# A planner with per-engine clocks in place of credits, attention sums through DRAM, and the residual's products moved ahead of the gates, in a one-core transformer block

## The chip, the cores and the metric

The kernel runs on one core of one Trainium2 chip. The metric is the device time of one execution in microseconds; the kernel before was run three times: 890.34, 892.4 and 892.6 us, median 892.4 us. The profile is of one further execution. Engines are named as in the profile: PE (matrix multiply), PEld (its weight loads), DVE (vector), ACT (scalar and activation), POOL (GpSimd), SP (the engine whose queue issues most of the DMAs).

## The reference, cut to what matters

The input is x of 8 batches, 512 tokens, 256 features, all in float32. The block is causal attention with 16 heads of 16 features, plus a "memory" term, then a residual and layer norm, then a mixture of 8 experts with the top 2 of 10 gates (two of them null), a residual and a second layer norm.

```
qkv = x @ qkv_w.T + qkv_b                      # 16 heads of 16
seq_out = softmax(causal(q k^T / 4)) v
lines   = exterior products of x and x shifted by one token, 6 numbers a head
M       = decayed sum over earlier tokens of outer(Jw, Jw)        # 6 x 6 a head
mem_score = mix of rd.M.rd and |rd.M|^2
gated   = mean over heads of sigmoid(mem_score * mem_scale) * sigmoid(x @ memg_w.T + memg_b)
x = layernorm(x + (seq_out + gated * (x @ memv_w.T + memv_b)) @ out_w.T + out_b)
w, sel = top_k(softmax(x @ gate_w.T + gate_b), 2)
x = layernorm(x + sum over e of w_e * (x @ expert_w[e] + expert_b[e]))
```

`gated` is one number a token, and it can be had only when the memory sums of all earlier tokens are done.

## The kernel before, in words

**Attention** is cut into 160 stints, ten for a pair of head groups (4 groups of 4 heads, 8 batches). Stint k computes two things (`products`, L202): plain scores of stint k (`mx`, L223), from which DVE takes each query's largest (`negmax` L258) while ACT copies the diagonal blocks out (`dia` L267), POOL masks them (L282) and DVE takes their largest a stint later (`negdia` L250); and, for the stint that is 8 behind (`LAG`), transposed scores with the largest already folded in (`sc`, L228), which ACT exponentiates (`pe`, L263) and POOL masks (L277). `mx` and `sc` have one buffer each of two PSUM banks, so that the next `mx` waits until `dia` is out. `values` (L296) multiplies `pe` with v, a column of ones beside it, into `po`.

**Attention's sums.** A group fills 32 rows for each of 4 heads: in groups with even number the first 16 rows are the sums and the next the denominator, in odd groups the other way round. ACT copies an even group's `po` to `osb` (L313), an odd one's to `raw`, and DVE merges it with a predicated copy (L316). The denominators alone (8 KB a group) go to DRAM (`den`, L314), come back spread over 128 partitions (`rec`, L323), are inverted on DVE (L325), go out again (`dr`, L327) and come back broadcast (`recs`, L664). POOL multiplies them in (L671).

**The other work** stands in Python generators: `memory` (lines, L399 to L442), `memory_sums` (64 rounds of two matmuls `pm` L560 with three DVE operations L568, L570, L550 and one POOL operation L531 each, 32 rounds for each half of the batches), `finish` and `memory_gate` (they end in `gated`), then for each batch `prepare` (L637: loads x, adds the output bias on POOL, multiplies in the denominators, and, once the gates of the half are known, adds gated * b2 on POOL, L676 and L677), `front` (L699: residual's products `pa` L708 and L711, added on DVE at L713 and L715, norm at L691, transposes `px`, gates of the experts) and `all_experts` (L803: 16 pairs of experts a batch, `pex` L827, each added by two DVE operations L831; then the second norm and the store).

**What sets the order.** The program order of every engine is fixed when the kernel is built (`in_this_order`). Between two stints `fill` (L900) runs generators on credit: a stint earns `TAKE` = 1.9 us less the price of what stands in it, plus 1.0 or 1.5; a generator yields the PE time that it used, or a word (`STEP`, `POOL`, `LESS`, `CALM`) that makes it go on at a later turn or when POOL has a share free. The prices are constants; no engine's load is followed. Credit that is not used becomes idle matmuls (`warm`, L894), one for each 0.3 us, which keep PE busy with nothing.

The last batches' experts run after the last stint.

Of the kernel before, what the change touches and what calls it, by code (L numbers as in the profile page):

```python
# [26 lines left out]
TAKE = 1.9  # L27
SB = 4
EARLY, MORE = 1.0, 1.5
WARM = 0.3  # L30
PV, PQ, PO = 1.2, 2.15, (1.05, 0.85, 0.65, 0.45)
ROUNDS = (2, 1)
BUCKET = 3
AHEAD = 6
HALF = 4
STEP, POOL, LESS = "goes on at the next turn", "needs GpSimd", "needs GpSimd for half as long"
CALM = "goes on at the next turn but a unit's last"
# [15 lines left out]
def in_pieces(op, *tiles):  # L53

    for c in range(0, NT, 2):
        op(*(t[:, c : c + 2] for t in tiles))
        yield STEP


def bc(ap, axis, n):  # L60

    ap = ap.unsqueeze(axis)
    shape = list(ap.shape)
    shape[axis] = n
    return ap.to_broadcast(shape)

# [12 lines left out]
def block_kernel(ctx, tc, x, xT, wqk, bqk, wtok, wod, memv, memvb, row, gw, we, eb, out):  # L79
    nc = tc.nc  # L80
    PS = bass.MemoryType.PSUM
    const = ctx.enter_context(tc.tile_pool(name="const", bufs=1))
    psA = ctx.enter_context(tc.tile_pool(name="psA", bufs=1, space=PS))
    psO = ctx.enter_context(tc.tile_pool(name="psO", bufs=1, space=PS))
    psB = ctx.enter_context(tc.tile_pool(name="psB", bufs=3, space=PS))
    att = ctx.enter_context(tc.tile_pool(name="att", bufs=2))
    dram = ctx.enter_context(tc.tile_pool(name="dram", bufs=2, space=bass.MemoryType.DRAM))
# [30 lines left out]
    memp = ctx.enter_context(tc.tile_pool(name="mem", bufs=1))  # L118
    lines_of = ExitStack()
    lp = lines_of.enter_context(tc.tile_pool(name="lines", bufs=2))  # L120
# [15 lines left out]
    make_identity(nc, ident)  # L136
# [12 lines left out]
    odd_rows = const.tile([P, 1], mybir.dt.uint8, name="odd_rows")  # L149
    nc.vector.tensor_copy(odd_rows, bq[:, 2 * NG + 1 : 2 * NG + 2])  # L150
# [145 lines left out]
    def values(u, *js):  # L296

        b, g = UNITS[u]
        if u not in pos:
            pos[u] = psO.tile([P, T], F32, tag="po", name=f"po{u}")  # L300
            begun[u] = set()
        for j in js:
            for h in range(4):
                nc.tensor.matmul(pos[u][32 * h : 32 * h + 32, j * P :], v_aug[b % 2][:, j, 4 * (g // 2) + h, g % 2 : g % 2 + 2].rearrange("p q d -> p (q d)"),  # L304
                                 pes[u, j, h // 2][:, h % 2], start=not begun[u], stop=len(begun[u]) == NT - 1)
            begun[u].add(j)
        if len(begun[u]) == NT:
            if g == 0:
                st[b]["osb"] = att.tile([P, KC, T], F32, name=f"osb{b}", tag="osb", bufs=3)
                st[b]["den"] = dram.tile([KC, 4, 2, T], F32, name=f"den{b}", tag="den")  # L310
            o = st[b]["osb"][:, g // 2, :]
            raw = att.tile([P, T], F32, name=f"raw{u}", tag="raw", bufs=1) if g % 2 else o
            nc.scalar.copy(raw, pos.pop(u))  # L313
            nc.sync.dma_start(st[b]["den"][g // 2, :, g % 2], raw[0 if g % 2 else DH :: 32])  # L314
            if g % 2:
                nc.vector.copy_predicated(o, odd_rows.to_broadcast([P, T]), raw)  # L316

    def invert(b, part):

        s = st[b]  # L320
        if part == 0:
            s["rec"] = att.tile([P, T // 8], F32, name=f"rec{b}", tag="rec", bufs=1)
            nc.sync.dma_start(s["rec"], s["den"].rearrange("k j q (e t) -> (k j q e) t", e=8))  # L323
        if part == 1:
            nc.vector.reciprocal(s["rec"], s["rec"])  # L325
            s["dr"] = dram.tile([KC, 8, T], F32, name=f"dr{b}", tag="dr")
            nc.sync.dma_start(s["dr"].rearrange("k j (e t) -> (k j e) t", e=8), s["rec"])  # L327


    def sigmoid(z):  # L330
# [3 lines left out]
        yield STEP  # L334
# [7 lines left out]
    def fold_values():  # L342

        wd, mv = wo, mv0
        for c in range(KC):
            pw = bank(f"pw{c}")
# [4 lines left out]
            yield 0.9  # L351
        for n in range(2):
            mbb = lp.tile([P, KC, P], F32, name="mbb")
# [8 lines left out]
            yield 0.9  # L362

    turned, lined, gates = set(), set(), set()
# [19 lines left out]
    def memory_later():  # L384
        for half in range(B // HALF):
            yield from memory_sums(half)

    finished, rounds = [], [0, 0]
    mem, lines_over = {}, []

    def lines(lp, b):
# [4 lines left out]
        for c in range(NT):  # L396
            pl = bank(f"pl{b}_{c}")
# [6 lines left out]
            yield 1.1  # L404

        nc.gpsimd.memset(s[0:1, 0, 0, : 4 * H], 0.0)
        nc.sync.dma_start(s[1:, :, 0, : 4 * H], w1[: P - 1])
        nc.sync.dma_start(s[0:1, 1:, 0, : 4 * H], w1[P - 1 :, : NT - 1])
        spawn(outer_lines(lp, b, s))

    def outer_lines(lp, b, s):
        t = mem[b // HALF]
        for _ in range(2):
            yield STEP
# [3 lines left out]
        yield POOL  # L418
# [5 lines left out]
        yield POOL  # L424
# [3 lines left out]
        yield POOL  # L428
# [3 lines left out]

        to = t["jw"][:, :, :, b % HALF, :6].rearrange("p c h k -> p c k h")
        nc.gpsimd.tensor_tensor(to[:, :, 0:3], lw[:, :, 0, 3:6], nw[:, :, 0, 3:6], ALU.subtract)
        nc.gpsimd.tensor_tensor(to[:, :, 3:6], lw[:, :, 0, 0:3], nw[:, :, 0, 0:3], ALU.subtract)
        yield STEP
        for v, o in ((t["rd"], t["rn"][:, :, :, b % HALF]), (t["jw"], t["jw"][:, :, :, b % HALF, 6])):
            sq = lp.tile([P, NT, H, 6], F32, name="sq", bufs=1)
            nc.scalar.activation(sq, v[:, :, :, b % HALF, :6], AF.Square)
            yield STEP  # L440
# [48 lines left out]
    def memory_ahead(half):  # L489
# [7 lines left out]
        yield STEP  # L497
        nc.vector.tensor_scalar(jl[96:, 0, :], jl[96:, 0, :], others[96:], None, ALU.mult)
        nc.sync.dma_start(jl[P - 1 :, 1:, :], dj[:, : NT - 1, :])
        yield STEP  # L500
        yield STEP
# [3 lines left out]
        yield POOL  # L505
# [4 lines left out]
        yield STEP  # L510
# [6 lines left out]
    def memory_sums(half):  # L517
# [24 lines left out]
        for n in range(AHEAD):  # L542
            outer(*todo[n])
            if n < 3:
                decay(*todo[n])
            if n % 2:
                yield STEP
# [5 lines left out]
        for n, (h, c) in enumerate(todo):  # L553
            h0 = h - h % 8
            if n % (4 * NT) == 0:
                rm = memp.tile([P, NT, 8 * HALF, 6], F32, tag="rm", name=f"rm{half}_{h0}", bufs=2)
            pm = bank(f"pm{half}_{h}_{c}")
# [6 lines left out]
            if n + AHEAD < len(todo):  # L564
                outer(*todo[n + AHEAD])
# [8 lines left out]
            yield 0.85  # L574
            if turn[0] != rounds[0]:
                rounds[:] = turn[0], 0
            rounds[1] += 1
            if rounds[1] >= ROUNDS[half]:
                yield STEP
            if n % (4 * NT) == 4 * NT - 1:  # L580
                sums(*behind)
                behind = None
                spawn(finish(half, h0, rm))

    def finish(half, h0, rm):
# [8 lines left out]
        for n, to, by in ((1, sm, of_heads), (2, sm2, rm)):  # L594
            for c in range(0, NT, 2):
                cs = slice(c, c + 2)
                yield LESS
# [5 lines left out]
        yield STEP  # L603
        nc.vector.tensor_reduce(*behind, AX.X, ALU.add)
        finished.append(half)
        if finished.count(half) == 2:
            spawn(memory_gate(half))

    def memory_gate(half):
        sm, sm2, rn, gexp = (mem[half][n] for n in ("sm", "sm2", "rn", "gexp"))  # L610
        if half == 0:
            al, be = memp.tile([P, 1], F32, name="al"), memp.tile([P, 1], F32, name="be")
            fac_of.update(al=al, be=be)
            nc.vector.tensor_copy(al, vec("mix"))
            yield from sigmoid(al)
            nc.vector.tensor_scalar(be, al, -1.0, 1.0, ALU.mult, ALU.add)
# [6 lines left out]
        yield STEP  # L623
# [3 lines left out]
        yield STEP  # L627
# [9 lines left out]
    def prepare(b):  # L637
        yield lambda: lines_over and b < left[0] + 3
        if not ffp:
            ffp.append(ctx.enter_context(tc.tile_pool(name="ff", bufs=2)))  # L640
# [9 lines left out]
        if len(ffp) == 2:  # L650
            ws = ffp[0].tile([P, KC, NTRUE, D], F32, name="ws", bufs=1)
            ffp.append(ws)
            for e in range(0, NTRUE, 2):
                for k in range(KC):
                    nc.sync.dma_start(ws[:, k, e : e + 2], we[e : e + 2, k * P : (k + 1) * P, :].rearrange("e p h -> p e h"))
                yield STEP
        for c in range(NT):
            yield LESS
            nc.gpsimd.tensor_tensor(xb[:, c], xb[:, c], ob2, ALU.add)
        yield lambda: b in done  # L660
        recs = []
        for k in range(KC):
            recs.append(ff.tile([P, T], F32, name=f"recs{b}_{k}", tag="recs"))
            nc.sync.dma_start(recs[k], bc(st[b]["dr"][k], 1, DH))  # L664
        yield STEP
        yield STEP
        for k in range(KC):
            for n in range(0, T, T // 2):
                yield LESS
                o = st[b]["osb"][:, k, n : n + T // 2]  # L670
                nc.gpsimd.tensor_tensor(o, o, recs[k][:, n : n + T // 2], ALU.mult)  # L671
        yield lambda: b // HALF in gates
        for c in range(NT):
            yield POOL
            gb2 = ff.tile([P, D], F32, tag="recs", name=f"gb2_{b}_{c}")
            nc.gpsimd.tensor_tensor(gb2, b2, gated[:, c, b : b + 1].to_broadcast([P, D]), ALU.mult)  # L676
            nc.gpsimd.tensor_tensor(xb[:, c], xb[:, c], gb2, ALU.add)  # L677
        yield STEP

    def root(mv, nm):  # L680

        n = mv.shape[1]
        rs = ffp[0].tile([P, NT], F32, tag="rs", name=f"rs_{nm}")
        nc.vector.tensor_scalar(rs[:, :n], mv[:, :, 1], EPS, None, ALU.add)  # L684
        rr = ffp[0].tile([P, NT], F32, tag="rr", name=f"rr_{nm}")
        nc.gpsimd.tensor_tensor(rr[:, :n], rs[:, :n], half[:, :n], ALU.pow)  # L686
        return rr

    def norm(out_t, in_t, mv, rr, c, r=None):
        r = c if r is None else r  # L690
        nc.vector.tensor_scalar(out_t[:, c, :], in_t[:, c, :], mv[:, c, 0:1], rr[:, r : r + 1],  # L691
                                ALU.subtract, ALU.mult)
# [6 lines left out]
    def front(b):  # L699

        yield lambda: b in prepared
        ff, osb, xb = ffp[0], st[b]["osb"], st[b]["xb"]
        y = xb
        mv = ff.tile([P, NT, 2], F32, tag="mv", name=f"mv1_{b}")
        for c in range(NT):
            pa = bank(f"pa{b}_{c}")
            for k in range(KC):
                nc.tensor.matmul(pa[:, D:], xt[:, b, k, c * P : (c + 1) * P], wt[:, k, CM : CM + D],  # L708
                                 start=(k == 0), stop=(k == KC - 1))
            for k in range(KC):  # L710
                nc.tensor.matmul(pa[:, :D], osb[:, k, c * P : (c + 1) * P], wo[:, k, :],  # L711
                                 start=(k == 0), stop=(k == KC - 1))
            nc.vector.scalar_tensor_tensor(y[:, c, :], pa[:, D:], gated[:, c, b : b + 1], xb[:, c, :],  # L713
                                           ALU.mult, ALU.add)
            nc.vector.tensor_tensor(y[:, c, :], y[:, c, :], pa[:, :D], ALU.add)  # L715
            stats(mv, y, c, f"a{b}")
            yield 1.9
        yield STEP
        x1 = y
        rr = root(mv, f"a{b}")  # L720
        yield STEP
        yield STEP
        for c in range(NT):
            norm(x1, y, mv, rr, c)
            if c % 2:
                yield STEP
        yield lambda: b < left[0] + 2
        x1T = ff.tile([P, KC, T], F32, tag="x1T", name=f"x1T_{b}")
        for k in range(KC):
            pt = bank(f"px{b}_{k}")  # L730
# [3 lines left out]
            yield 0.7  # L734

# [7 lines left out]
        yield 0.6  # L743
        yield STEP
# [8 lines left out]
        yield 0.3  # L753
        yield CALM
# [8 lines left out]
        for r in range(2):  # L763
# [16 lines left out]
            yield CALM  # L780
# [4 lines left out]
        yield CALM  # L785
# [9 lines left out]
        yield CALM  # L795
# [7 lines left out]
    def all_experts(b):  # L803
# [4 lines left out]
        yield STEP  # L808
# [5 lines left out]
        yield 0.4  # L814
# [219 lines left out]
```

## Time and profile before

| | us |
|---|---|
| median of 3 runs | 892.4 |
| the profiled execution | 894.46 |
| its span, first to last instruction | 892.7 |
| PE busy, and its idle matmuls (L898) alone | 810.6, 40.0 |
| DVE, ACT, POOL busy | 633.0, 365.3, 390.6 |
| last exponential of attention (L263) ends | 737.4 |
| first expert product (L827) starts | 372 |

A group of instructions is read as: line, engine, operation, what it writes and reads, shape, count; then the busy time of the group in us, the mean of one in ns; then the idle time of the engine just before these instructions, and what ended most of it. The clock that is granted to PE is a share of full speed; its mean over the span is 0.973.

### The profile page before, as it was taken

What the parts mean: (1) busy time and instruction counts of PE and PEld (TensorE: products, weight loads), DVE (VectorE), ACT (ScalarE), POOL (GpSimd) and SP (SyncE); (2) the same over time, 40 slices, a digit from 0 to 9 for tenths busy, and PEclk for the clock granted to TensorE, in tenths of its full rate; (3) what the DMA queues carried; (4) which work ended last, traced back from release to release, by engine and by line L of the source; (5) the groups of instructions that cost most, each with busy time, mean ns of one, the idle gap of its engine ahead of it and who ended that gap; (6) DMA issues with size and microseconds to landing.
All of it is one profiled execution on the core that took longest, in us unless ns stands there. A gap on an engine that the chain in (4) does not pass through costs nothing.

```text
span 892.7 us, 14145 instructions
## 1 busy us (share of the span) xinstructions
PE 810.6 (91%) x5102; PEld 444.6 (50%) x5102; DVE 633.0 (71%) x1431; ACT 365.3 (41%) x678; POOL 390.6 (44%) x695
## 2 busy tenths in 40 slices
PE   9999977887779998999898899999999998999997
PEld 5555545454546555644364346444644454545342
DVE  2445579897579677878576778766876847887765
ACT  4466664554545464353445354544454321000000
POOL 1265777584646496642133463344334425050000
PEclk9999998998999998999899999999999999999999
DMA  7000000300000010000001000020002002020000
GB/s 267 12 17 17 9 3 3 123 24 1 5 1 26 27 28 25 2 4 1 2 1 51 26 1 1 15 63 2 1 7 70 2 1 75 1 71 1 24 30 18
DMA packets 25846, 23.70 MB, mean 27 GB/s; under 512 B 8588, under 2 KB 21548, under 8 KB 25776
## 3 DMA queue, kind: packets, MB, share of 16 engines
q1 hardware_dynamic: 24432, 22.24, 8.1%
q8 instruction: 40, 0.66, 0.3%
q10 hardware_dynamic: 1344, 0.56, 0.2%
q14 instruction: 30, 0.25, 0.1%
HBM read 16.75 MB, written 4.73 MB: 24 GB/s over the span
## 4 chain that ended last, share of the span: by engine, by line
PE 63%; DVE 19%; ACT 6%; POOL 5%; issue 4%; DMA 2%; SPq 1%; POOLq 0%; ACTq 0%; DVEq 0%
PE pex L827 22%; PE mx L223 8%; PE pq L167 6%; PE po L304 6%; PE sc L228 6%; PE pa L708 3%; PE pa L711 3%; DVE negmax L258 3%; PE pl L399 3%; DVE x L831 2%; DVE negdia L250 2%; PE pv L177 2%; ACT dia L267 2%; ACT pe L263 2%; DVE ou L568 2%
## 5 line engine op out<-in xcount | busy, mean ns | idle before, releaser
L827 PE MATMUL pex<-ws,x1T 128*128 128x512 f32 x512 | 239.4, 610 | 14.3 <-DVE x L842 5.9
L263 ACT ACTIVATE pe<-sc 128x1024 f32<-128x1024 f32 x160 | 164.0, 1025 | 215.9 <-PE sc L228 193.2
L223 PE MATMUL mx<-qk,qk 32*128 32x384 f32 (+3 forms) x1024 | 190.1, 472 | 44.0 <-ACT dia L267 43.9
L277 POOL TENSOR_SCALAR_AFFINE_SELECT pe<-pe 128x256 f32<-128x256 f32 (+1 forms) x224 | 97.5, 449 | 280.3 <-ACT pe L263 279.9
L258 DVE TENSOR_REDUCE negmax<-mx 128x2 f32<-128x768 f32 (+2 forms) x160 | 126.8, 793 | 100.0 <-PE sc L228 56.5
L228 PE MATMUL sc<-qk,qk 32*128 32x384 f32 (+3 forms) x1024 | 187.7, 472 | 1.8 <-DMA qk<-nt 1.8
L831 DVE SCALAR_TENSOR_TENSOR x<-pex,cw,x 128x256 f32<-128x256 f32 x256 | 123.0, 480 | 68.2 <-PE pex L827 62.1
L827 PEld LDWEIGHTS pex<-ws,x1T 128*128 128x128 f32 x512 | 93.1, 192 | 124.9 <-issue 97.2
L223 PEld LDWEIGHTS mx<-qk,qk 32*128 32x128 f32 x1024 | 79.3, 188 | 112.8 <-ACT dia L267 74.7
L282 POOL TENSOR_SCALAR_AFFINE_SELECT dia<-dia 128x512 f32<-128x512 f32 (+1 forms) x160 | 90.2, 564 | 76.9 <-ACT dia L267 74.4
L267 ACT COPY dia<-mx 128x512 f32<-128x512 f32 (+1 forms) x160 | 79.9, 499 | 74.8 <-DVE negmax L258 70.5
L228 PEld LDWEIGHTS sc<-qk,qk 32*128 32x128 f32 x1024 | 89.0, 188 | 24.7 <-issue 3.5
L250 DVE TENSOR_REDUCE negdia<-dia 128x4 f32<-128x512 f32 (+1 forms) x160 | 91.3, 570 | 6.1 <-POOL dia L282 6.0
L304 PE MATMUL po<-pe,v_aug 128*32 128x512 f32 (+3 forms) x1024 | 88.6, 453 | 0.2 <-POOL pe L277 0.2
L167 PE MATMUL pq<-xt,wq 128*128 128x512 f32 x128 | 66.4, 644 | 0.7 <-DMA xt<-in_xT 0.7
L304 PEld LDWEIGHTS po<-pe,v_aug 128*32 128x32 f32 x1024 | 25.4, 110 | 57.0 <-issue 38.0
L560 PE MATMUL pm<-ou,dm 128*128 128x144 f32 x256 | 48.0, 319 | 3.2 <-DVE pr L570 2.8
L171 ACT ACTIVATE qk<-pq,bq 128x512 f32<-128x512 f32 x64 | 46.3, 775 | 11.0 <-PE pq L167 10.7
L686 POOL TENSOR_TENSOR rr_b<-rs_b,half 128x4 f32<-128x4 f32 (+1 forms) x11 | 9.3, 847 | 85.8 <-DVE rs_b L684 85.7
L560 PEld LDWEIGHTS pm<-ou,dm 128*128 128x128 f32 x256 | 38.1, 203 | 17.2 <-issue 10.0
L531 POOL TENSOR_TENSOR ou<-jw,jf 128x288 f32<-128x288 f32 x64 | 44.3, 700 | 1.3
L898 PE MATMUL idle<-ident 128*128 128x128 f32 x246 | 40.0, 309 | 1.5 <-POOL ident masks.py:199 1.5
(168 smaller groups left out, 967.1 us busy)
## 6 DMA issues: line engine op xcount, KB each, us to landing
xt<-in_xT SPq DMA_DIRECT2D x8, 512.0 KB
x<-in_x SPq DMA_DIRECT2D x8, 512.0 KB
recs<-dr SPq DMA_DIRECT2D x16, 256.0 KB
out_y<-x SPq DMA_DIRECT2D x32, 128.0 KB
ws<-in_we SPq DMA_DIRECT2D x8, 256.0 KB
s<-w SPq DMA_DIRECT2D x8, 127.0 KB
qk<-nt ACTq DMA_DIRECT2D x32, 8.0 KB
wq<-in_wqk SPq DMA_DIRECT2D x3, 128.0 KB
```

The lines of the kernel that those rows point to most:

```text
L167: nc.tensor.matmul(pq, wq[:, k, w, g // 2, :], xt[:, b, k, :], start=(k == 0), stop=(k == KC - 1))
L223: nc.tensor.matmul(mx[:, h, c : c + n], qk[m, 0][r, n - P : n], qk[m, 1][r, :n], start=True, stop=True)
L228: nc.tensor.matmul(sc[:, h, c : c + n], qk[v, 1][r, j * P : (j + 1) * P], qk[v, 0][r, j * P :], start=True, stop=True)
L250: nc.vector.tensor_reduce(out_, in_, AX.X, ALU.max, negate=True)
L258: nc.vector.tensor_reduce(to, rest, AX.X, ALU.max, negate=True)
L263: nc.scalar.activation(pe, sc, AF.Exp, scale=DH**-0.5)
L267: nc.scalar.copy(dia[:, :, :nd], diag)
L277: nc.gpsimd.affine_select(out=tri, in_=tri, compare_op=ALU.is_ge, fill=0.0, base=0, pattern=[[0, tri.shape[1]], [1, P]], channel_multiplie ...
L282: nc.gpsimd.affine_select(out=inside, in_=inside, compare_op=ALU.is_ge, fill=MASKED, base=0, pattern=[[0, 2 * nd], [-1, P]], channel_multi ...
L304: nc.tensor.matmul(pos[u][32 * h : 32 * h + 32, j * P :], v_aug[b % 2][:, j, 4 * (g // 2) + h, g % 2 : g % 2 + 2].rearrange("p q d -> p (q ...
L827: nc.tensor.matmul(pe, x1T[:, k, c * P : (c + 1) * P], ws[:, k, 2 * ep : 2 * ep + 2, :].rearrange("p e h -> p (e h)"), start=(k == 0), sto ...
L831: nc.vector.scalar_tensor_tensor(x1[:, c, :], pe[:, e * D : (e + 1) * D], cw[:, c, 2 * ep + e : 2 * ep + e + 1], x1[:, c, :], ALU.mult, AL ...
```

## The change

It has four parts.

1. **The order.** Credits and their constants go. A class `Pace` notes every instruction as it is recorded and keeps an estimated time for PE, DVE, ACT, POOL and SP, for each buffer the time at which it is free, and for each tile the time at which it is done. A generator now yields an `Ask`: tiles that must be done, engines whose estimated time may be at most a given step past PE's (`SPARE`: 0.8 us DVE, 0.9 ACT, 3.0 POOL), and whether matmuls follow (then a PSUM bank must be free). `fill` goes through the generators by rank: sums of the memory first, then lines, preparations, fronts, experts. It fills until the time at which `mx` and `sc` are free, or longer where the experts still to come are to be spread over the stints that are left. What is left of the wait becomes idle matmuls. The sums of the memory may now have one or more rounds a stint, as DVE and POOL allow.
2. **Attention sums through memory.** Every group's `po` is copied to `raw`, and all 128 rows (256 KB) go to DRAM (`heads`). DVE's predicated copy is gone. The denominators are read out of `heads` by four DMAs, and inverted ones written by four. In `prepare` 16 DMAs read the sums back into place (each 16 partitions of four runs of 512 bytes), before the two broadcast loads of `recs`.
3. **Residual's products ahead of the gates.** The `pa` matmuls move from `front` to `prepare`. DVE adds the attention half to x, ACT copies the memory half to `osb`'s place (32 new copies of 128x256), POOL adds b2 to that (32 operations in the place of L676 and L677). When the gates are known, one DVE operation a token tile (in L713's form, from SBUF) does the rest.
4. **The norms** go from DVE (L691, 64 operations) to ACT as scale and bias; for it DVE negates the means and POOL multiplies them (19 small operations each).

```diff
+class Pace:
+    HAND, OVER = {"DVE": 0.033, "Activation": 0.033, "Pool": 0.07, "PE": 0.04, "SP": 0.03}, {"DVE": 0.08, "Activation": 0.1, "Pool": 0.04}
+    LANDS = {"s": 9.9, "recs": 3.9, "x1": 3.9, "ws": 4.5}
...
+        elif op == "DMACopy":
+            start = max(self.at[e], t)
+            self.at[e] = start + (0.05 if e == "SP" else 0.45)
...
+            end = start + (self.LANDS.get(slot[1], 1.7) if start > 1.0 else 7.0)
...
-            raw = att.tile([P, T], F32, name=f"raw{u}", tag="raw", bufs=1) if g % 2 else o
+            raw = att.tile([P, T], F32, name=f"raw{u}", tag="raw", bufs=2)
             nc.scalar.copy(raw, pos.pop(u))
-            nc.sync.dma_start(st[b]["den"][g // 2, :, g % 2], raw[0 if g % 2 else DH :: 32])
-            if g % 2:
-                nc.vector.copy_predicated(o, odd_rows.to_broadcast([P, T]), raw)
+            nc.sync.dma_start(st[b]["heads"][g], raw)
...
+        osb = st[b]["osb"] = ff.tile([P, NT, KC, P], F32, tag="osb", name=f"osb{b}")
+        for g in range(NG):
+            of = st[b]["heads"][g].rearrange("(j q d) t -> j q d t", q=2, d=DH)[:, g % 2]
+            for j in range(4):
+                at = 32 * j + DH * (g % 2)
+                nc.sync.dma_start(osb[at : at + DH, :, g // 2, :], of[j].rearrange("d (c t) -> d c t", c=NT))
...
+            yield Ask(*(() if c else (xb, osb)), products=True, on=V + S)
             pa = bank(f"pa{b}_{c}")
...
+            nc.vector.tensor_tensor(xb[:, c], xb[:, c], pa[:, :D], ALU.add)
+            nc.scalar.copy(of_memory(b, c), pa[:, D:])
+        for c in range(NT):
+            yield ON_G
+            nc.gpsimd.tensor_tensor(of_memory(b, c), of_memory(b, c), b2, ALU.add)
...
-        nc.vector.tensor_scalar(out_t[:, c, :], in_t[:, c, :], mv[:, c, 0:1], rr[:, r : r + 1],
-                                ALU.subtract, ALU.mult)
+        nc.scalar.activation(out_t[:, c, :], in_t[:, c, :], AF.Identity, bias=mv[:, c, 0:1], scale=rr[:, r : r + 1])
...
+    def may(ask, over, slack):
...
+        now = pace.at["PE"]
+        late = max(now, until[0])
+        by = now + 0.2 if ask.products else late + LATE
+        if ask.after and over > late + LATE or any(pace.done(t.name) > by for t in ask.of):
+            return False
+        if any(pace.at[e] > late + slack + SPARE[e] for e in ask.on):
+            return False
+        return not ask.products or now < until[0] + slack and pace.free("psB", "bank", 3) < now + 0.2
...
+        banks = [pace.free("psA", n, 1) for n, on in (("mx", k + 1 < STINTS), ("sc", 0 <= kv + 1 < STINTS)) if on]
+        share = max(FILL * (B - 1 - left[0]) - TAIL, 0.0) / max(STINTS - kv, 1) if ready else 0.0
...
+        least = max(banks, default=0.0)
+        least -= sum(sum(PO[j] for j in js) + 0.2 for _, js in due(kv + 1))
+        fill(max(least, began + share), least)
+        began = pace.at["PE"]
```

## The prediction

> **What bounds the kernel now.** I read the busy times first, then PE's groups with the idle time before them, then the busy times in stretches cut where each tenth stint's exponential starts, then the waits, then SP's queue. The first view says that PE is the engine to look at:
>
> ```profile
> PE 810.6 (91%) x5102; PEld 444.6 (50%) x5102; DVE 633.0 (71%) x1431; ACT 365.3 (41%) x678; POOL 390.6 (44%) x695
> ```
>
> Of PE's groups three matter, and of DVE's those that the change takes away:
>
> ```profile
> L827 PE MATMUL pex<-ws,x1T 128*128 128x512 f32 x512 | 239.4, 610 | 14.3 <-DVE x L842 5.9
> L223 PE MATMUL mx<-qk,qk 32*128 32x384 f32 (+3 forms) x1024 | 190.1, 472 | 44.0 <-ACT dia L267 43.9
> L898 PE MATMUL idle<-ident 128*128 128x128 f32 x246 | 40.0, 309 | 1.5 <-POOL ident masks.py:199 1.5
> ...
> L691 DVE TENSOR_SCALAR x<-x,mv,rr_a 128x256 f32<-128x256 f32 x32 | 14.7, 502 | 0.0
> ...
> L316 DVE COPY_PREDICATED osb<-odd_rows,raw 128x512 f32<-128x512 uint8 x16 | 12.6, 786 | 22.0 <-ACT raw L313 22.0
> ```
>
> The reader is to see that 40.0 of PE's 810.6 us are idle matmuls. So the work itself is 770.6 us, and 892.7 - 810.6 = 82.1 us are gaps, 44.0 of them before `mx`, which waits for the diagonal's copy. Who holds that copy up is told by the waits (engine, line, for whom; us, times, longest):
>
> ```profile
> ACT dia L267 <- DVE negmax L258: 70.5, 62, 4.3
> ```
>
> It is DVE. Where, the stretches tell (busy us of PE, PEld, DVE, ACT, POOL with instruction counts; PE's clock; DMA):
>
> ```profile
> 84.00:123.00 39.00, 35.56 (x285) 21.74 (x284) 26.42 (x45) 25.02 (x52) 26.09 (x41) 1.00 0.04 8
> 123.00:168.00 45.00, 33.24 (x263) 20.34 (x262) 38.78 (x73) 23.18 (x41) 32.99 (x56) 0.89 0.07 23
> 168.00:215.00 47.00, 38.70 (x285) 23.86 (x286) 41.60 (x83) 22.98 (x41) 32.19 (x56) 0.90 0.17 51
> 215.00:256.00 41.00, 32.58 (x266) 20.44 (x266) 24.78 (x50) 21.33 (x37) 22.39 (x41) 0.91 0.01 4
> ...
> 694.00:737.00 43.00, 42.61 (x228) 21.03 (x229) 27.27 (x75) 13.78 (x17) 16.33 (x29) 1.00 0.01 2
> 737.00:893.00 156.00, 141.16 (x482) 67.75 (x481) 116.07 (x321) 6.49 (x18) 29.58 (x43) 1.00 0.10 31
> ```
>
> From 123 to 256 us PE is idle 28.5 of 133 us, at a clock of 0.9, while the memory's sums crowd DVE (86% and 89%). From 694 on PE is full. So **the gaps lie in the first half, and the last 156 us are expert work that found no place earlier**.
>
> **The sum, term by term.** Counting both programs by kind, PE has the same matmuls but for the idle ones: 123 before, 197 after. All terms are of the profiled span.
>
> - *Work: 770.6 us.* Some of it was stretched by the clock: PE busy 104.5 us from 123 to 256 at 0.9, 43 and 45 us from 331 to 378 and 424 to 472 at 0.93 each, 43 us from 472 to 521 at 0.97, so about 10 + 6 + 1 = 17 us. If smaller gaps give half of it back, -8 (bounds -17 and 0).
> - *Idle matmuls: +54.* From 84 to 123 us 24 of them took 6.58 us, 0.27 each; 197 x 0.27 = 54 (64 at the mean over the span, 40.0 / 123).
> - *Gap before mx: 44 becomes 20.* The planner holds DVE work back that would run more than 0.8 us past the point at which `mx` is wanted, and DVE loses 12.6 us (L316) and 27.1 us (both norms, 14.7 + 12.4), less 19 negations at 0.16 (row L467: 0.147; L616: 0.156). But the 64 rounds keep their 0.46 + 0.44 + 0.53 us of DVE each, and the norms and new copies go into ACT's queue, where the diagonal's copy stands: 64 x 0.42 + 32 x 0.37 = 39 us (rows 0.416 for an activation, 0.374 for a PSUM copy of 128x256). ACT as a whole has room, at 365 + 39 of 875; but one of these just ahead of the diagonal costs its 0.4 us. Bounds 0 and 44; I take a little under half, as the planner's fixed order meets real durations.
> - *Gaps before pex, pt, pg, pm: 27 becomes 14.* They are 14.3 + 5.5 + 4.0 + 3.2, the first in the tail, where DVE is 74% busy. Of 256 expert matmuls 128 stand behind the last transposed scores before, 72 after, and the norms leave DVE. Bounds 5 and 27.
> - *Start, end, rest: 11 stay.* 82.1 - 44.0 - 27.0; the end alone, after PE's last matmul, is 5.8.
> - *POOL* loses L676 and L677 (19.9 + 23.3), gains 32 additions (0.73 each as L677: 23) and 19 small products (0.1 to 1.0 each; the power of the same size took 0.85 to 1.02): at 44% it hides this. Cost 0.
> - *The trip through DRAM* is on no path while stints run, if it has time. SP's queue gives its prices (start, length, instruction):
>
> ```profile
> 303.40 0.50 SPq L314 DMA_DIRECT2D den<-raw  x1
> 305.21 0.32 SPq L323 DMA_DIRECT2D rec<-den  x1
> 305.63 1.26 SPq L664 DMA_DIRECT2D recs<-dr  x2
> ```
>
>   A write is read back 1.81 us after its issue; an issue takes 0.32 to 0.63 us (0.29 the shortest, L645). Yet the planner counts 0.05 us for an SP issue. From the reciprocal on, SP issues 4 writes (1.3), 16 loads (16 x 0.4 = 6.4; 4.6 to 10.1 by the shortest and longest row), 2 broadcasts (1.3); the second of these landed 4.0 us after its issue where two went out at 339.40 (packets to 344.12). That is 13.0 us (11.2 to 16.7). In the new order the first POOL product stands 2, 3, 2, 6, 15, 11 and 3 stints behind the reciprocal for batches 0 to 6. At 4.3 us a stint, batches 0 and 2 are short by 4.4 us each. POOL then waits, with masks of `pe` and `dia` behind it, which PE wants a stint later: half reaches PE, +4 (bounds 0 and 40, all batches late by 5 to 6).
> - *The last batch's trip: +8.* No stint hides it: copy 0.6, write and read back 1.8, four reads 1.3 + 1.4, reciprocal 0.5, then 13.0 and one product 0.7, in all 19.3. PE's order has 10 idle matmuls and 10 expert ones (7.1 us for 8 of them) and a bias there: 12 us. Bounds 0 and 19.
>
> 770.6 - 8 + 54 + 20 + 14 + 11 + 4 + 8 = **873.6 us of span**. The execution was 1.8 us longer than its span, and the median of the runs 2.1 us below it: 873 us, 2.2% less.
>
> **The skill beside the rows.** The Trainium skill, "DMA: Bandwidth & Descriptors", Anatomy of one DMA, speaks against the detour: about 2 us fixed for each DMA plus bytes at 436 GB/s, mostly the write's receipt, worst into HBM. For 256 KB that would be an estimated 2.6 us in the place of the measured 1.81, 0.8 us more at the end. "TensorE: Matmul & The Clock Gate", The HAM clock gate, says that PE falls to half speed after an idle window of about 3.4 us; the 0.9 seen from 123 us on agrees, and if the planner leaves no such window, all 17 us come back and the sum is 9 lower.
>
> **Rivals.**
> 1. *The planner hits.* Gaps before `mx` 5, the four others 5, clock -17, no waits for DRAM but 4 at the end: 770.6 - 17 + 54 + 5 + 5 + 11 + 4 = 833; anything to 858 counts here. For it: before 84 and after 521 us, where DVE is below 80%, gaps are small already. Against: fixed order against real jitter.
> 2. *The change does not do what it says.* DVE bounds the memory's stretches whatever the order, the 44 us stay, only more idle matmuls stand beside them: 873 + 24 = 897; with part of it, 888 to 898. For it: 41.60 of 47 us. Against: it is two stretches of seventeen.
> 3. *Slower: SP's queue.* If the 16 loads hold POOL up in every batch, PE's masks and `pa` come late by 5 us in the seven batches under stints: 873 + 35 = 908. It decides from 2.4 us a batch (17 us in all), that is, where the trip exceeds the stints left for it. For it: 0.05 in the plan against 0.32 or more in the trace. Against: five of seven batches have 3 stints or more.
>
> **Chances.** Forecast (858 to 888) 0.44, rival 1 0.23, rival 2 0.13, rival 3 (898 to 915) 0.20. Leaving out the lower half of rival 1 and of rival 3 the upper half gives 848 to 907. A measurement of this kernel tells 0.3%, 2.7 us, from nothing. Faster: 0.44 + 0.23 and a little of rival 2, 0.69; same 0.08; slower 0.23.
>
> **What would show it.** Right: the gap before `mx` near 20; idle matmuls near 54 us; first `pex` near stint 54 (before: 79); the clock above 0.95 in every stretch; DVE near 597 and ACT near 404. SP: 16 loads taking about 6.4 us a batch; POOL waiting for `recs` at batches 0 and 2 only; PE standing some 8 us before the last batch's `pa`. Wrong: POOL's products of `osb` waiting in most batches, or the same 44 us before `mx`, or expert matmuls waiting for DVE in the crowded stints from 120 on, where 22 to 28 of them now stand in ten stints instead of 12 to 20.

## The result, and the profile after

The changed kernel takes 917.2 us (median of 4 runs, 914.9 to 920.2) where the kernel before, beside it, takes 891.4 us: a ratio of 1.030, 95% interval 1.026 to 1.034. It is slower by 3.0%; 2.2% faster was forecast, and the time lies above the range given (848 to 907).

The head of the page of the changed kernel. DVE and ACT are about as busy as was forecast (597 and 404):

```profile
span 915.5 us, 14833 instructions
...
PE 826.0 (90%) x5250; PEld 459.8 (50%) x5250; DVE 593.6 (65%) x1369; ACT 404.0 (44%) x774; POOL 375.2 (41%) x682
```

Its groups. Every operation goes through the planner's wrapper, so all lines are L189, and groups are told by tiles:

```profile
L189 PE MATMUL pex<-ws,x1T 128*128 128x512 f32 x512 | 242.9, 609 | 0.2 <-DVE x L189 0.2
L189 PE MATMUL mx<-qk,qk 32*128 32x128 f32 (+3 forms) x1024 | 188.5, 470 | 16.0 <-ACT dia L189 13.4 <-ACT qk L189 2.1
L189 PE MATMUL idle<-ident 128*128 128x128 f32 x394 | 59.4, 294 | 15.7 <-DVE pr L189 3.9 <-DVE x L189 3.0 <-ACT gexp L189 2.4
L189 PE MATMUL pm<-ou,dm 128*128 128x144 f32 x256 | 43.4, 302 | 8.4 <-DVE pr L189 7.9 <-ACT v_aug L189 0.5
L189 PE MATMUL pa<-wo,osb 128*128 128x256 f32 x128 | 35.3, 397 | 9.7 <-POOL osb L189 9.7
L189 POOL TENSOR_TENSOR osb<-osb,recs 128x256 f32<-128x256 f32 x32 | 22.9, 726 | 75.6 <-DMA recs<-dr 62.5 <-issue 13.1
L189 PE MATMUL pt<-ident,negdia 128*16 128x128 f32 x32 | 9.2, 288 | 25.0 <-DVE negdia L189 22.3 <-DVE x L189 1.5 <-ACT gexp L189 0.9
```

The planner's aim is met where it was looked for: the gap before `mx` fell from 44.0 to 16.0 us, that before the expert products from 14.3 to 0.2, and the first expert product starts at 297 us, not 372. But POOL stood 75.6 us before its products of `osb`, which did not wait at all before, and the gaps before `pt` (25.0), `pm` (8.4) and `pa` (9.7) have grown. The same groups in the kernel before:

```profile
L671 POOL TENSOR_TENSOR osb<-osb,recs 128x256 f32<-128x256 f32 x32 | 22.5, 729 | 0.0
L288 PE MATMUL pt<-ident,negdia 128*16 128x128 f32 x32 | 9.3, 290 | 5.5 <-DVE negdia L256 4.8 <-ACT x1T L733 0.6
L560 PE MATMUL pm<-ou,dm 128*128 128x144 f32 x256 | 48.0, 319 | 3.2 <-DVE pr L570 2.8 <-ACT pe L263 0.5
L711 PE MATMUL pa<-wo,osb 128*128 128x256 f32 x128 | 32.9, 379 | 0.0
```

One such wait of the changed kernel, of batch 1, in the order of time (start, length, engine, instruction; in brackets the idle time before it and who ended it):

```profile
257.37 0.64 POOL L189 TENSOR_SCALAR_AFFINE_SELECT dia<-dia 128x512 f32<-128x512 f32 x1
...
262.40 1.38 SPq L189 DMA_DIRECT2D recs<-dr  x2
...
266.45 0.72 POOL L189 TENSOR_TENSOR osb<-osb,recs 128x256 f32<-128x256 f32 x1 [8.44 <-DMA recs<-dr]
...
268.13 0.63 POOL L189 TENSOR_SCALAR_AFFINE_SELECT dia<-dia 128x512 f32<-128x512 f32 x1
...
268.79 0.69 DVE L189 TENSOR_REDUCE negdia<-dia 128x4 f32<-128x512 f32 x1 [7.26 <-POOL dia L189]
...
270.18 0.38 PE L189 MATMUL pt<-ident,negdia 128*16 128x128 f32 x1 [8.35 <-DVE negdia L189]
```

POOL comes to the product 8.44 us before the broadcast has landed. A diagonal's mask is queued behind it; DVE's `negdia` waits for the mask, with the next `negmax` behind it; PE's `pt` waits for `negdia`. PE stands 8.35 us for a product that it needs much later. What SP did meanwhile:

```profile
241.41 0.33 SPq L189 DMA_DIRECT2D heads<-raw  x1
241.79 2.77 SPq L189 DMA_DIRECT2D rec<-heads  x4
248.76 2.61 SPq L189 DMA_DIRECT2D dr<-rec  x4
251.41 10.88 SPq L189 DMA_DIRECT2D osb<-heads  x16
262.40 1.38 SPq L189 DMA_DIRECT2D recs<-dr  x2
```

The 16 loads take 10.88 us to issue, 0.68 each, and the broadcasts that POOL waits for are issued behind them. The planner counted 16 x 0.05 = 0.8 us.

The last view is the stretches of three of these waits (busy us of PE, PEld, DVE, ACT and POOL, then PE's clock and the DMA columns):

```profile
144.00:194.00 50.00, 37.85 (x297) 23.94 (x297) 35.67 (x72) 19.70 (x30) 26.78 (x46) 0.86 0.25 85
234.00:275.00 41.00, 30.93 (x278) 17.73 (x275) 25.75 (x54) 21.46 (x35) 20.06 (x37) 0.88 0.13 41
314.00:360.00 46.00, 37.23 (x272) 17.91 (x269) 24.93 (x56) 22.08 (x37) 15.15 (x30) 0.89 0.12 37
```

Each holds one wait (batches 0, 1 and 2): 8.4 to 9.2 us of POOL, and 7.1 to 8.4 us of PE behind it. In each the granted clock is 0.86 to 0.89, so that the matmuls around the wait take longer as well; by how much is shown with e2_few below.

### The profile page after: what moved, and what is told of

Read it like the earlier page. It is cut to its first block, busy times and chain, and to the rows that moved or that the text cites. A ratio compares the mean times of both kernels' runs of the same rounds, so it can differ in the third digit from the quotient of the medians.

```text
span 915.5 us, 14833 instructions
## 1 busy us (share of the span) xinstructions
PE 826.0 (90%) x5250; PEld 459.8 (50%) x5250; DVE 593.6 (65%) x1369; ACT 404.0 (44%) x774; POOL 375.2 (41%) x682
## 4 chain that ended last, share of the span: by engine, by line
PE 55%; DVE 13%; SPq 9%; POOL 7%; issue 7%; DMA 6%; ACT 3%; ACTq 0%; POOLq 0%; DVEq 0%
PE pex L189 19%; SPq L189 9%; PE mx L189 7%; PE po L189 6%; PE pa L189 6%; PE sc L189 5%; PE pq L189 4%; DMA recs<-dr 3%; PE pv L189 2%; DVE x L189 2%; DVE negdia L189 2%; DVE negmax L189 2%; PE idle L189 1%; POOL dia L189 1%; POOL ln L189 1%
## 5 line engine op out<-in xcount | busy, mean ns | idle before, releaser
L189 ACT ACTIVATE pe<-sc 128x1024 f32<-128x1024 f32 x160 | 163.8, 1024 | 193.7 <-PE sc L189 179.9
L189 PE MATMUL pex<-ws,x1T 128*128 128x512 f32 x512 | 242.9, 609 | 0.2 <-DVE x L189 0.2
L189 POOL TENSOR_SCALAR_AFFINE_SELECT pe<-pe 128x256 f32<-128x256 f32 (+1 forms) x224 | 97.4, 449 | 294.8 <-ACT pe L189 294.4
L189 PE MATMUL mx<-qk,qk 32*128 32x128 f32 (+3 forms) x1024 | 188.5, 470 | 16.0 <-ACT dia L189 13.4
L189 DVE TENSOR_REDUCE negmax<-mx 128x2 f32<-128x768 f32 (+2 forms) x160 | 126.9, 793 | 103.6 <-PE sc L189 55.9
L189 DVE SCALAR_TENSOR_TENSOR x<-pex,cw,x 128x256 f32<-128x256 f32 x256 | 123.2, 481 | 99.7 <-PE pex L189 94.7
L189 PE MATMUL sc<-qk,qk 32*128 32x384 f32 (+3 forms) x1024 | 186.9, 468 | 0.9 <-ACT pe L189 0.8
L189 PEld LDWEIGHTS pex<-ws,x1T 128*128 128x128 f32 x512 | 93.0, 193 | 99.0 <-issue 91.1
L189 PEld LDWEIGHTS mx<-qk,qk 32*128 32x128 f32 x1024 | 78.5, 188 | 83.8 <-ACT dia L189 37.3
L189 POOL TENSOR_SCALAR_AFFINE_SELECT dia<-dia 128x512 f32<-128x512 f32 (+1 forms) x160 | 88.4, 553 | 65.5 <-ACT dia L189 62.2
L189 ACT COPY dia<-mx 128x512 f32<-128x512 f32 (+1 forms) x160 | 79.8, 499 | 74.0 <-DVE negmax L189 73.4
L189 DVE TENSOR_REDUCE negdia<-dia 128x4 f32<-128x512 f32 (+1 forms) x160 | 91.1, 569 | 27.0 <-POOL dia L189 27.0
L189 PEld LDWEIGHTS sc<-qk,qk 32*128 32x128 f32 x1024 | 89.3, 187 | 23.3 <-issue 4.3
L189 PE MATMUL po<-pe,v_aug 128*32 128x512 f32 (+3 forms) x1024 | 91.1, 464 | 2.1 <-POOL pe L189 2.1
L189 PE MATMUL idle<-ident 128*128 128x128 f32 x394 | 59.4, 294 | 15.7 <-DVE pr L189 3.9
L189 PEld LDWEIGHTS idle<-ident 128*128 128x128 f32 x394 | 51.2, 200 | 27.0 <-issue 10.6
L189 PE MATMUL pq<-xt,wq 128*128 128x512 f32 x128 | 63.3, 618 | 0.9 <-DMA xt<-in_xT 0.9
L189 PEld LDWEIGHTS po<-pe,v_aug 128*32 128x32 f32 x1024 | 26.0, 112 | 58.2 <-issue 39.3
L189 POOL TENSOR_TENSOR osb<-osb,recs 128x256 f32<-128x256 f32 x32 | 22.9, 726 | 75.6 <-DMA recs<-dr 62.5
L189 PE MATMUL pm<-ou,dm 128*128 128x144 f32 x256 | 43.4, 302 | 8.4 <-DVE pr L189 7.9
L189 ACT ACTIVATE qk<-pq,bq 128x512 f32<-128x512 f32 x64 | 46.2, 774 | 10.8 <-PE pq L189 10.8
L189 PEld LDWEIGHTS pm<-ou,dm 128*128 128x128 f32 x256 | 36.7, 194 | 23.6 <-issue 11.0
```

Source lines behind the costliest of these rows:

```text
L189: i = made(*args, **kwargs)
```

## The experiments

Theory 1: the trip through DRAM takes far longer than the planner thinks; products are placed on POOL as if the data were there, and the masks behind them hold DVE and PE up. Theory 2: the new order itself loses. Theory 3: the additional DMAs do harm by themselves. All times are medians beside the kernel before on the same chip; that one's medians were 889.1, 886.6 and 889.2 us in the three groups of runs, so a difference between runs of two groups is sure to some 3 us only.

**The planner told the truth about SP (e1_price).**

```diff
-            self.at[e] = start + (0.05 if e == "SP" else 0.45)
+            self.at[e] = start + (0.66 if e == "SP" else 0.45)
```

> The changed kernel, but the planner counts 0.66 us for a DMA issue of SP, as the trace of it shows (16 loads in 11.08 us), in the place of 0.05; the order is planned anew, nothing else differs. Theory 1 (the trip through DRAM is slower than planned; POOL waits for it with masks behind, and PE for those): POOL's 75.6 us of waits before the products of osb fall under 15, PE's gap before pt (22.3) under 6; but 307 idle matmuls are planned in the place of 197, 110 x 0.27 = 30 us more, so the time is about 917 - 40 + 24 = 901 us. Theory 2 (the new order as such loses, in the first ten stints and at the end, whatever the trip costs): 915 us or more, and the gaps that go come back as idle matmuls to the full.

909.1 us, ratio 1.024 (1.019 to 1.028), 8 us more than theory 1 expected. POOL's waits under the stints are gone (24.2 us is left, all at the last batch), and PE's gap before `pt` falls from 25.0 to 16.2 us (9.3 of it for `negdia`, where under 6 was expected). But idle matmuls rise from 59.4 to 85.6 us, those after the last exponential from 15.2 to 31.8. Between the two theories: the waits were due to the plan, yet planning for so long a trip turns much of them into planned idling.

**Fewer issues (e2_few).** Odd groups' rows are stored over those of even groups, denominators go out on their own and come back in one DMA, their inverses are written by one, and one load of 128 partitions remains for each half of `osb`. The order of instructions on POOL, DVE and ACT is that of the changed kernel.

```diff
-            nc.sync.dma_start(st[b]["heads"][g], raw)
...
+            nc.sync.dma_start(st[b]["den"][g // 2, :, g % 2], raw[0 if g % 2 else DH :: 32])
+            if g % 2:
+                for j in range(4):
+                    r = slice(32 * j + DH, 32 * j + 2 * DH)
+                    nc.sync.dma_start(st[b]["heads"][g // 2, r], raw[r])
+            else:
+                nc.sync.dma_start(st[b]["heads"][g // 2], raw)
...
-        for g in range(NG):
...
-                nc.sync.dma_start(osb[at : at + DH, :, g // 2, :], of[j].rearrange("d (c t) -> d c t", c=NT))
+        for k in range(KC):
+            nc.sync.dma_start(osb[:, :, k, :], st[b]["heads"][k].rearrange("p (c t) -> p c t", c=NT))
```

> The changed kernel in the same planned order, but the trip has fewer issues where it is waited for: odd groups' rows are written over the even group's in DRAM by four stores during the stints, denominators go out on their own, and after the reciprocal one write, two loads of 128 partitions and two broadcasts remain (5 issues in the place of 22). Theory 1: the trip from the reciprocal on takes about 7 us in the place of 19, POOL's waits before the products of osb fall from 75.6 to under 10 us, PE's gaps before pt, pm and pa from 39.9 to under 8, the time to 880 us (872 to 890). Theory 2: gaps there close, but the time stays over 905 us.

868.5 us, ratio 0.979 (0.974 to 0.984): faster than both kernels, and faster than the 872 to 890 that theory 1 expected. The new order does not lose by itself: theory 2 falls. The matmuls, the idle ones too, are as many as in the changed kernel. SP's queue at batch 1, in the form of the fence above:

```profile
238.76 0.34 SPq L189 DMA_DIRECT2D dr<-rec  x1
239.14 1.32 SPq L189 DMA_DIRECT2D osb<-heads  x2
240.56 1.25 SPq L189 DMA_DIRECT2D recs<-dr  x2
```

From the write of the reciprocals to the last broadcast's issue SP is busy 3.1 us, where the changed kernel takes 15.0. The two loads, of 128 partitions and 256 KB each, take 0.66 us each to issue, about as much as each of the 16 small ones: SP's time went with the number of loads here, not with their bytes. The page's line of engines, and the groups that had waited:

```profile
PE 810.0 (94%) x5250; PEld 453.5 (52%) x5250; DVE 592.3 (69%) x1369; ACT 404.4 (47%) x774; POOL 375.7 (43%) x682
```

```profile
L189 PE MATMUL pm<-ou,dm 128*128 128x144 f32 x256 | 42.8, 299 | 1.3 <-DVE pr L189 0.7 <-ACT v_aug L189 0.5
L189 PE MATMUL pa<-wo,osb 128*128 128x256 f32 x128 | 32.8, 379 | 0.0
L189 POOL TENSOR_TENSOR osb<-osb,recs 128x256 f32<-128x256 f32 x32 | 23.1, 734 | 13.8 <-DMA recs<-dr 13.8
L189 PE MATMUL pt<-ident,negdia 128*16 128x128 f32 x32 | 8.8, 274 | 11.5 <-DVE negdia L189 8.5 <-DVE x L189 1.5 <-ACT gexp L189 1.2
```

The 13.8 us are one wait, at the last batch, where PE does not suffer (0.0 before `pa`); under 10 was expected. PE's busy time without idle matmuls is 810.0 - 57.8 = 752.2 us, against 766.6 in the changed kernel, with the same work: the mean clock is 0.995 against 0.965. The stretch of batch 1 shows it, 31 us where it had been 41, at full clock, with 28.73 us of PE in the place of 30.93:

```profile
224.00:255.00 31.00, 28.73 (x277) 17.04 (x273) 25.19 (x53) 21.46 (x35) 20.16 (x37) 1.00 0.17 51
```

**Norms on DVE again (e3_norm)**, planned anew, in the changed kernel otherwise.

```diff
-        nc.vector.tensor_scalar(mv[:, :, 0], mv[:, :, 0], -1.0, None, ALU.mult)
...
-        nc.gpsimd.tensor_tensor(mv[:, :, 0], mv[:, :, 0], rr[:, :n], ALU.mult)
...
-        nc.scalar.activation(out_t[:, c, :], in_t[:, c, :], AF.Identity, bias=mv[:, c, 0:1], scale=rr[:, r : r + 1])
+        nc.vector.tensor_scalar(out_t[:, c, :], in_t[:, c, :], mv[:, c, 0:1], rr[:, r : r + 1],
+                                ALU.subtract, ALU.mult)
```

> The changed kernel with the norms on DVE again, as before (64 operations of DVE, none of the 19 negations and products); planned anew, with 257 idle matmuls in the place of 197. Theory 1: the trip stays as slow, POOL waits 60 us or more for it, and the time is 917 + 10 to 20 us, as DVE is fuller. Theory 2 (in the form that ACT is the harmed engine, since it waited 57.2 us for POOL's mean products, longest 10.2): 905 us or less.

932.7 us, ratio 1.051 (1.046 to 1.056). POOL still waits 68.9 us. The norms in ACT's queue are not what harms.

**No trip for the sums (e4_keep).** Groups are merged in SBUF by DVE again, and only the denominators go through DRAM; planned anew.

```diff
-            raw = att.tile([P, T], F32, name=f"raw{u}", tag="raw", bufs=2)
...
+            o = st[b]["osb"][:, g // 2, :]
+            raw = att.tile([P, T], F32, name=f"raw{u}", tag="raw", bufs=1) if g % 2 else o
             nc.scalar.copy(raw, pos.pop(u))
...
+            nc.sync.dma_start(st[b]["den"][g // 2, :, g % 2], raw[0 if g % 2 else DH :: 32])
+            if g % 2:
+                nc.vector.copy_predicated(o, odd_rows.to_broadcast([P, T]), raw)
```

> The changed kernel without the trip of the sums: groups are merged in SBUF with DVE's predicated copy, only denominators go through DRAM (the old way), and the memory half of the products takes the place of the sums in SBUF. The planner, the products ahead of the gates and the norms on ACT stay; 252 idle matmuls in the place of 197. Theory 1: POOL's waits before the products of osb under 10 us, 917 - 40 + 15 = 892 us, about the time of before. Theory 2: 905 us or more.

890.7 us, ratio 1.0035 (1.001 to 1.006), 26 us less than the changed kernel, as theory 1 has it. It is 22 us more than e2_few: idle matmuls 74.5 us against 57.8, and DVE 602.0 us against 592.3. So the detour is worth having, if it is short.

**The same trip in the old order (e5_old_dram).** The kernel before with the 16 loads and the rest of the trip:

```diff
...
-            if g % 2:
-                nc.vector.copy_predicated(o, odd_rows.to_broadcast([P, T]), raw)
...
+            nc.sync.dma_start(st[b]["heads"][g], raw)
...
+                nc.sync.dma_start(osb[at : at + DH, :, g // 2, :], of[j].rearrange("d (c t) -> d c t", c=NT))
```

> The kernel before with the trip of the sums through DRAM alone, in the changed kernel's form (16 loads a batch, four reads and writes of denominators); the old order, the products behind the gates and the norms on DVE stay. Theory 1 (not the trip as such costs, but that products are placed behind it as if it took 4.8 us): in the old order POOL's products follow the broadcasts' issue by 5 to 16 us, so POOL's waits before them stay under 25 us in all, and the time stays within 10 us of before (880 to 900), with DVE 12 us less busy. Theory 3 (22 more DMAs a batch harm by themselves, by contention or through SP's order): 910 us or more.

885.8 us, ratio 0.998 (0.995 to 1.002). POOL waits 28.1 us, a little over what was expected, PE 3.0 before `pa`. With the same DMAs and the same bytes there is no loss: theory 3 falls. (DVE, without its merge, is busy 614.9 us in the place of 633.0, so that a loss of a few us may be hidden; theory 3 expected 910 us or more.)

**The suspected cost doubled (e6_double).**

```diff
-                nc.sync.dma_start(osb[at : at + DH, :, g // 2, :], of[j].rearrange("d (c t) -> d c t", c=NT))
+                for n in range(0, NT, 2):
+                    nc.sync.dma_start(osb[at : at + DH, n : n + 2, g // 2, :], of[j].rearrange("d (c t) -> d c t", c=NT)[:, n : n + 2])
```

> The changed kernel in the same order with the suspected cost doubled: 32 loads a batch of 16 KB in the place of 16 of 32 KB, the bytes the same. Theory 1: 16 more issues of 0.6 to 0.7 us make the trip 10 to 11 us longer; POOL's waits before the products of osb rise from 75.6 to about 75 + 8 x 10.5 = 160 us, and half to all of what is new reaches PE: 960 to 1000 us. Theory 3 (bytes or DRAM, not issues): under 925 us.

964.1 us, ratio 1.088 (1.083 to 1.094). The time is as expected, but by another sum: 32 loads issue in 16.11 us, not 22, as a smaller load issues faster (0.50 against 0.68 each), and POOL waits 42.6 us more, not 85:

```profile
L189 POOL TENSOR_TENSOR osb<-osb,recs 128x256 f32<-128x256 f32 x32 | 22.9, 726 | 118.2 <-DMA recs<-dr 106.7 <-issue 11.5
```

So all of it reaches the end (47 us for 42.6), a part by the clock (0.942 against 0.965).

**Which batches pay (e9_last_only, e10_not_last).** Both forms of the trip in one kernel; the short one for batches 0 to 6, or for the last alone:

```diff
+            if b < B - 1:          # e9_last_only; in e10_not_last: b == B - 1
+                nc.sync.dma_start(s["rec"], s["den"].rearrange("k j q (e t) -> (k j q e) t", e=8))
+            else:
                 for g in range(NG):
...
                     nc.sync.dma_start(s["rec"][32 * g : 32 * g + 32], ones)
```

> The version with few issues for batches 0 to 6; the last batch alone keeps the changed kernel's trip with 16 loads. It tells what the long trip costs where no stint hides it. In the changed kernel PE stood 7.0 us before the last batch's products more than in the version with few issues, and the stretch after the last exponential was 114.6 us against 99.9: 868.5 + 7 to 15, about 879 us. If the last trip is hidden by experts, under 871 us.

881.8 us, ratio 0.992 (0.988 to 0.995): the last batch's long trip costs 881.8 - 868.5 = 13.3 us.

> The reverse: the last batch has few issues, batches 0 to 6 keep the 16 loads. POOL waits 50 us before their products (9.2, 8.4, 9.1, 4.7, 7.8, 6.5, 5.0). The share of the stints: 917 - 868.5 less the last batch's part, 34 to 42 us, so about 906 us. If POOL's waits in the stints are mostly hidden, as the prediction had it for five of these batches, under 880 us.

905.5 us, ratio 1.019 (1.013 to 1.026): the seven others cost 905.5 - 868.5 = 37.0 us. The two make 50.3 us, the two kernels differ by 917.2 - 868.5 = 48.7: within the spread of the groups, nothing is left over.

**What the other parts are worth without the waits.** The norms on DVE in e2_few (e7_few_norm, the diff of e3_norm):

> The version with few issues (odd rows written over even ones in DRAM, two loads a batch), but with the norms on DVE as before the change; planned anew, 233 idle matmuls in the place of 197. What the norms on ACT are worth without the trip's waits: by the first experiments 36 x 0.27 = 10 us of idle matmuls and some us more, so about 880 us against 868.5. If the norms on ACT are worth nothing or harm (ACT waits 57 us for their factors), 868 us or less.

880.9 us, ratio 0.994 (0.991 to 0.998): the norms on ACT are worth 12.3 us. The products held back until the gates are known, in e2_few (e11_gates):

```diff
+        yield lambda: b // HALF in gates
         for c in range(NT):
             yield Ask(*(() if c else (xb, osb)), products=True, on=V + S)
...
-        yield lambda: b // HALF in gates
```

> The version with few issues, but the residual's products wait for the gates of their half again (their place in the code, and all operations, stay as changed); planned anew, 209 idle matmuls in the place of 197. If running ahead of the gates matters beyond the plan's 12 idle matmuls (3 us), 880 us or more; if the gates come early enough anyway, 868 to 874 us.

885.0 us, ratio 0.997 (0.994 to 1.000): products ahead of the gates are worth 16.5 us, more than the idle matmuls that they save (63.4 us against 57.8); the rest was not taken apart. The planner's constant, in e2_few (e8_few_tail, `TAIL` 55 in the place of 70):

> The version with few issues, with the planner's constant for the work left behind the last stint at 55 in the place of 70; planned anew, 191 idle matmuls in the place of 197. Six idle matmuls are 2 us: 864 to 872 us, no difference that can be told from 868.5. It tells whether the constant, tuned for the changed kernel, is off for this one.

869.6 us, ratio 0.981 (0.976 to 0.987): no difference that can be told.

## Why the prediction was wrong, step by step

The forecast's terms, beside what the two traces show (us; idle time is taken from the groups, the rest is the difference to the span):

| term | forecast | changed kernel | e2_few |
|---|---|---|---|
| work of PE | 762.6 | 766.6 | 752.2 |
| idle matmuls | 54 | 59.4 | 57.8 |
| gap before mx | 20 | 16.0 | 14.7 |
| gaps before pex, pt, pg, pm, with what POOL's waits bring | 14 + 4 | 33.6 | 12.8 |
| gap before pa, last trip | 8 | 9.7 | 0.0 |
| start, end, rest | 11 | 30.2 | 26.4 |
| span | 873.6 | 915.5 | 863.9 |

- *Gaps before mx and pex*: right, and a little better than forecast. The planner does what it says; rival 2 falls.
- *Idle matmuls*: 0.30 each in the place of 0.27. Right in kind.
- *The load moved to ACT and POOL costs nothing*: no run shows a cost; with the norms back on DVE both planned kernels are slower, by 15.5 us (e3_norm) and 12.3 us (e7_few_norm).
- *The trip under stints, +4: the step that failed.* It was called short for batches 0 and 2 alone, since the first POOL product stands 6, 15, 11 and 3 stints behind the reciprocal for batches 3 to 6. But that is not where the trip starts. `prepare` of a later batch is held until earlier batches have left, and issues the 16 loads then: 14, 58, 50 and 10 us after the reciprocal for batches 3 to 6. The planner puts the product as far behind these loads as it thinks they take (4.8 us: 18 issues of 0.05 and 3.9 to land), in every batch. POOL came to it 6 to 10 us after the first load's issue, and the product could begin after 14 to 15. So POOL waited in all seven: 9.2, 8.4, 9.1, 4.7, 7.8, 6.5 and 5.0 us, 50.7 in sum, 24.0 of it in batches 3 to 6. The distance should have been counted from the loads. Batch 4 shows it (SP's queue, then POOL; the reciprocal had ended at 497.55):

```profile
497.57 2.59 SPq L189 DMA_DIRECT2D dr<-rec  x4
...
555.47 10.23 SPq L189 DMA_DIRECT2D osb<-heads  x16
565.80 1.39 SPq L189 DMA_DIRECT2D recs<-dr  x2
...
569.59 0.72 POOL L189 TENSOR_TENSOR osb<-osb,recs 128x256 f32<-128x256 f32 x1 [7.84 <-issue]
```

- *Its length, 13.0 (11.2 to 16.7)*: 17.7 to 18.0 us from the reciprocal's end to the product in batches 0 to 2, so that the three stints of batch 1 (12.9 us) were too few as well. Loads issued at 0.68 each, not 0.4, and four small writes took 2.6 us, not 1.3. The upper bound, from the longest issue shown (0.63), was too low as well.
- *Half reaches PE*: more than half, 37.0 of 50.7, as e10_not_last shows, and part of it through the clock (PE is busy 820.3 us there, in e2_few 810.0, with the same matmuls).
- *The last trip, +8*: 13.3, right in kind; PE stood 9.7 us before `pa`. With the seven others the trip cost 50.3 us, 38 more than the 12 forecast; the median is 44 above the forecast.
- *Rest, 11 stay*: 30.2, of which 15.7 are short waits that the planner leaves ahead of its idle matmuls; these were not thought of. They stand in e2_few too (16.2), so they are no part of the loss against it; against the forecast this term is 19 us off.
- *A reading*: PE was called full from 694 us on, and the gap before `pex` was put into the tail. The line of 737 to 893 shows PE 90% busy (141.16 of 156), and of the 14.3 us before `pex` 7.7 stand there. The sum does not suffer.
- *Rival 3* was the case: it priced the seven batches at 35 us, and they cost 37.0. Its time (908, to 915 at most) still fell short of 917.2, because it kept the forecast's other terms, the rest (11) above all. The case for it was in the text, 0.05 in the plan against 0.32 or more in the trace, and it was set aside by the wrong distance.
- *The forecast and e2_few*: with the trip made short the time is 868.5 us, 4.5 below the forecast, which already held 12 us for the trip. That it comes so near is in part luck: in the span the rest is 15.4 us above its term, which the work (10.4 below) and the gaps make up for.
- *The clock*: in e2_few it came back almost whole (mean 0.995; the work took 752.2 us against 770.6 before, a little past the bound of -17). The Trainium skill, "TensorE: Matmul & The Clock Gate", The HAM clock gate, puts the half clock behind an idle window of about 3.4 us. The traces agree on the half clock, but not on the length of the wait: from 123 to 256 us the kernel before ran six times at 0.5 for 3.4 to 6.8 us, with one wait of PE above 3.4 us among them (4.66), and e2_few, whose longest wait of PE is 2.4 us, still has two such stretches, at 40.3 and 118.8 us.
- *The skill's price of a DMA*: the section that the prediction names is headed as the path of the gpsimd engine, while the trip's DMAs are issued by SP. No run here measured a 256 KB write by itself, and the sum did not use the price.

What stays open: the changed kernel reaches its tenth exponential at 96.7 us where the kernel before did at 83.9, and e2_few at 95.2. No run took that apart. Nor is it shown what makes one issue take 0.34 us and another 0.68; the number of bytes is not it (e2_few).

## What to carry to other kernels

A planner that fixes the order is as good as its worst price: one that is too low puts the consumer ahead of its data in an in-order queue, and everything behind it pays, here a mask on POOL that PE waits for by way of DVE. Before such a plan is trusted, set its price for each resource beside the same instruction in a trace, the issuing queue of DMAs among them, and count a consumer's distance from the instruction that starts the transfer, not from the value that it carries. If the price is right and the trip still long, make the trip short: the planner with true prices gained 8 us, merged transfers 49. Both together were not tried.

## What the runs showed of the hardware that was not expected

Sixteen loads of 32 KB (16 partitions of four runs of 512 bytes) took SP 10.9 us to issue, 0.68 each, while a store of 256 KB out of 128 partitions took 0.33; 32 loads of 16 KB took 0.50 each, and two loads of 256 KB (128 partitions of four runs of 512 bytes) 0.66 each. So here more bytes did not mean a longer issue: eight times the partitions with the same runs cost SP the same, and a load cut in two took 1.5 times as long to issue, not twice.

Waits of 7.1 to 8.4 us on PE came with a clock of 0.86 to 0.89 over the 41 to 50 us around them. Without these waits (e2_few) the clock was 1.00 in the same stretches, and the same matmuls took 14.4 us less of PE in the whole span. In batch 1 a wait of 8.35 us went with a stretch 10 us longer (41 against 31): it cost more than its length.
